# Clearing an idle tile on GpSimd ahead of every sixth gather of a graph network's second layer

## The chip, the cores and the metric

The kernel runs on one core of one Trainium2 chip. The core has five engines that run side by side and wait for each other through semaphores: TensorE (PE; PEld is its weight load), VectorE (DVE), ScalarE (ACT), GpSimd (POOL) and SyncE (SP). Data moves between the off-chip memory and the on-chip memory (SBUF) through 16 DMA engines. A DMA is issued by one of the engines: plain transfers here by SP, gathers and scatters by index (indirect DMAs) by POOL. An engine works through its own instructions strictly in order.

The metric is the device time of one execution in microseconds (us); lower is better.

## The reference

The input is a graph of 10,000 nodes with 768 numbers each and 170,000 edges (80,000 random pairs in both directions, and a self loop for each node), sorted by target. Two layers of graph attention with residual products and normalisations follow, and a last normalisation:

```python
def gat_conv(x, edge_index, W, a_src, a_dst, bias, heads, out_ch, concat):
    ei = _add_self_loops(edge_index, n)
    src, dst = (ei[0], ei[1])
    xl = (x @ W).reshape(n, heads, out_ch)
    alpha_src = jnp.einsum('nhc,hc->nh', xl, a_src)
    alpha_dst = jnp.einsum('nhc,hc->nh', xl, a_dst)
    e = jax.nn.leaky_relu(alpha_src[src] + alpha_dst[dst], 0.2)
    m = jax.ops.segment_max(e, dst, num_segments=n)
    e = jnp.exp(e - m[dst])
    s = jax.ops.segment_sum(e, dst, num_segments=n)
    alpha = e / (s[dst] + 1e-16)
    msg = xl[src] * alpha[:, :, None]
    out = jax.ops.segment_sum(msg, dst, num_segments=n)
    ...
h = gat_conv(x, edge_index, W1, a_src1, a_dst1, b1, HEADS, HID, True)    # 4 heads of 256
h = jax.nn.relu(layer_norm(h, g1, be1))
h = h1 = h + (x @ Wr1 + br1)                                             # 1024 numbers a node
h = gat_conv(h, edge_index, W2, a_src2, a_dst2, b2, 1, OUT_DIM, False)   # 1 head of 768
h = layer_norm(h, g2, be2) + (h1 @ Wr2 + br2)
return _layernorm(x + h)
```

For each node this is a weighted mean over the rows of its neighbours, with weights that depend on both ends of the edge. All of it is in float32.

## The kernel before, in words

**Stages.** First the edges are sorted into lists and the nodes ordered by their number of neighbours, while TensorE makes the table of layer 1 (up to about 950 us). Then layer 1 runs over 79 tiles of 128 nodes and writes each tile's row of table2: 770 numbers a node (768 of the product with W2, two of the attention). Then layer 2 runs over the same 79 tiles and writes the output. The change is in layer 2 alone.

**Slots.** Since nodes of one tile have nearly the same number of neighbours, a tile has SLOTS[t] places of 128 rows, one row for each of its 128 nodes: 41 for the tile with most neighbours, then 27, 26 and so on down to 8. Over all tiles these are TOTAL = 1377 places, numbered q. The tiles' turns go from the short ones up to the 41-slot tile (turn 39) and from 27 down to 9 again. In layer 2 the first place of each tile holds the tile's own rows, which one plain DMA from SP loads (L474); each of the other 1298 is one gather of 128 rows by POOL (L477, in the helper at L445). The places of a tile are its single ones (1 to 4) and blocks of four (a "wave"). Each gather moves 128 x 770 x 4 bytes, 394 KB.

**The ring.** The gathered rows lie in a ring of 41 slots in SBUF. `fetch(upto)` (L471) issues the loads of all places up to a given one, in order. A gather waits until the slot's rows of 41 places earlier have been used.

**One turn of layer 2** (L1077 to L1104), in the order in which it is written out by hand (the schedule is manual, so each engine's instructions run in this order):

1. `exponents(t)`: DVE reads the attention numbers out of the tile's rows (L960 is its first instruction) and ACT takes the exponential (L994).
2. the first part of `norms` of the tile before on DVE (L1048 to L590).
3. `weighed(t)`: DVE makes the weight blocks (`spots`, L1005) and sums the single rows in SBUF (L1014 the first, L1012 the others). L1014 writes one of two row buffers, which the scatter of the tile two turns before must have left.
4. POOL and SP: `ring.fetch` of the places that the singles made free (L1082).
5. second part of `norms` (L601, L603, L604, L1056), which adds the residual product.
6. PE: the blocks of four (`summed`, L1026) between the residual products of the next tile (`residual`, L1036 and L1038).
7. last part of `norms` of the tile before: ACT writes the normalised rows (L1062), POOL scatters them to the output by node number (L1063).
8. POOL and SP: `ring.fetch` of the places that the blocks made free (L1100); SP loads the residual's inputs of the turn after next (L927, L928).

So POOL's queue in layer 2 holds nothing but the gathers (L445), one scatter a tile (L1063) and one small IOTA (L943), in that order: gathers for the singles, the scatter of the tile before, gathers for the blocks.

Of the kernel before, what the change touches and what calls it, by code (L numbers as in the profile page):

```python
# [28 lines left out]
F32 = mybir.dt.float32  # L29
# [6 lines left out]
P = 128  # L36
BANK = 512
# [41 lines left out]
def gnn_kernel(ctx, tc, x, x_cols, src, dst, src_col, dst_col, W1, a_src1, a_dst1, b1, g1, be1, Wr1, br1,  # L79
               W2, a_src2, a_dst2, b2, g2, be2, Wr2, br2, out, n_edges):  # L80
    nc = tc.nc
# [362 lines left out]
    def gather(to, table, index, **more):  # L444
        nc.gpsimd.indirect_dma_start(out=to, out_offset=None, in_=table,  # L445
                                     in_offset=bass.IndirectOffsetOnAxis(ap=index, axis=0), **more)
# [14 lines left out]
    class Ring:  # L461
# [4 lines left out]
        def __init__(self, pool, table, row, size, own, index, more=0):  # L466
            self.table, self.size, self.own, self.issued, self.index = table, size, own, 0, index
            self.row = row
            self.rows = pool.tile([P, size, row + more], F32, name="ring")

        def fetch(self, upto):  # L471
            for q in range(self.issued, min(upto, TOTAL)):
                if q in self.own:
                    nc.sync.dma_start(self.slot(q)[:, :self.row],  # L474
                                      self.table[self.own[q] * P:(self.own[q] + 1) * P, :])
                elif q < self.size or self.own:
                    gather(self.slot(q)[:, :self.row], self.table[:, :], self.index(q))  # L477
                else:
                    gather(self.slot(q)[:, :self.row], self.table[:, :], self.index(q), bounds_check=NP - 1,
                           oob_is_err=False)  # L480
                self.issued = q + 1
# [895 lines left out]
```

## Time and profile before

| | |
|---|---|
| median of 3 runs | 5389.56 us (5383.51 to 5395.65) |
| the profiled execution's own time | 5383.51 us |
| its span, from first to last instruction | 5381.6 us |
| POOL busy | 3296.9 us (61% of the span), 3160 instructions |
| PE / DVE / ACT busy | 4604.0 / 3856.7 / 2741.2 us |
| layer 2: first gather starts, last gather starts, last scatter starts | 3445.03, 5313.94, 5369.81 us |
| moved by DMA in the whole | 1591 MB, mean 296 GB/s |

How to read the lines of the profile shown below. The page cuts the span into 40 equal slices and gives each engine's busy share of a slice in tenths. A table by stage gives the busy time of each engine in a stretch of the span, with the number of instructions in brackets, the clock that TensorE was granted, the share of time that the DMA engines were busy, and what they moved. A group of instructions has its line, engine and operation, the tile written and the tile read, partitions x elements, the count; then busy time and mean ns of one; then the idle time before them and what ended it. The timeline gives start and length of each instruction in us, and in brackets the engine's idle time before it and who released it ("issue": nothing that the profile shows). In the waits, a line reads "who waits <- for whom: us in all, times, longest". Issuing a DMA from POOL counts as busy time of POOL (DMA_INDIRECT); the transfer itself runs on the DMA engines afterwards.

### The profile page before, as it was taken

How to read it: one execution, taken by the hardware profiler on the slowest of the kernel's cores; microseconds unless marked ns; L12 is line 12 of the kernel's file. 1: busy time of each engine (PE TensorE's matmuls, PEld its weight loads, DVE VectorE, ACT ScalarE, POOL GpSimd, SP SyncE). 2: the span in 40 equal slices, each digit the busy share in tenths (PEclk: the TensorE clock that was granted, in tenths of full speed). 3: DMA queues.
4: the chain of work that ended last, by engine and by line, in shares of the span. 5: the costliest groups of instructions: out<-in, count | busy, mean ns of one | idle time of the engine just before them, and what ended most of it. 6: DMA issues, size and time to landing. Idle time of an engine off the chain costs nothing. (4 is left out here: it accounts for less than half of the span.)

```text
span 5381.6 us, 61043 instructions
## 1 busy us (share of the span) xinstructions
PE 4604.0 (86%) x16999; PEld 2427.2 (45%) x16999; DVE 3856.7 (72%) x8213; ACT 2741.2 (51%) x6878; POOL 3296.9 (61%) x3160
## 2 busy tenths in 40 slices
PE   8999996999999887578999999788877766778887
PEld 3444443555555544345555555444433322333343
DVE  5884254899999887788899999577655433465677
ACT  3434443787888876778888888322211111111122
POOL 3446455555666664656666555267777767777774
PEclk9999998999999988789999999899998878889899
DMA  4333625899999996789999999589999989999995
GB/s 155 125 98 88 92 93 213 300 339 345 358 357 368 356 343 248 288 331 346 358 370 354 354 336 321 198 305 359 355 352 352 347 281 343 343 349 356 367 358 224
DMA packets 474309, 1591.47 MB, mean 296 GB/s; under 512 B 118327, under 2 KB 122487, under 8 KB 473958
## 3 DMA queue, kind: packets, MB, share of 16 engines
q0 software_dynamic: 322384, 1286.62, 65.7%
q1 hardware_dynamic: 149520, 297.43, 16.1%
q10 hardware_dynamic: 2054, 3.42, 0.2%
q8 instruction: 137, 2.24, 0.2%
q14 instruction: 214, 1.75, 0.1%
HBM read 1431.80 MB, written 177.29 MB: 299 GB/s over the span
## 5 line engine op out<-in xcount | busy, mean ns | idle before, releaser
L445 POOL DMA_INDIRECT ring<-table,slots x1495 | 1520.0, 1017 | 1012.0 <-issue 230.3
L445 POOL DMA_INDIRECT ring<-table,wide x1180 | 1196.2, 1014 | 387.6 <-issue 189.1
L532 ACT ACTIVATE ring<-ring,e 128x256 f32<-128x256 f32 x3284 | 1337.9, 510 | 0.0
L539 DVE TENSOR_TENSOR acc<-acc,ring 128x1024 f32<-128x1024 f32 x801 | 985.7, 1231 | 79.1 <-ACT ring L532 10.1
L1038 PE MATMUL big<-wr,w 128*128 128x512 f32 (+1 forms) x2464 | 888.0, 509 | 0.0
L179 PE MATMUL big<-w,xT 128*128 128x512 f32 x1896 | 825.7, 597 | 23.3 <-DMA w<-in_W_dram 9.7
L179 PE MATMUL big<-wr,xT 128*128 128x512 f32 x1896 | 833.6, 596 | 0.2 <-ACT xT L715 0.2
L832 PE MATMUL half<-w,hT 128*128 128x512 f32 (+1 forms) x2528 | 830.4, 486 | 0.0
L543 DVE SCALAR_TENSOR_TENSOR acc<-ring,e,acc 128x256 f32<-128x256 f32 x1232 | 602.3, 489 | 82.4 <-PE acc L744 43.0
L1026 PE MATMUL acc<-ring,spots 128*32 128x512 f32 (+1 forms) x4720 | 471.6, 534 | 215.6 <-issue 176.6
L744 PE MATMUL acc<-ring,diagonals 128*128 128x256 f32 x1912 | 483.3, 411 | 200.8 <-ACT diagonals L738 200.5
L1038 PEld LDWEIGHTS big<-wr,w 128*128 128x128 f32 x2464 | 482.1, 198 | 371.6 <-issue 340.6
L832 PEld LDWEIGHTS half<-w,hT 128*128 128x128 f32 x2528 | 477.8, 189 | 372.8 <-issue 310.4
L179 PEld LDWEIGHTS big<-w,xT 128*128 128x128 f32 x1896 | 361.7, 192 | 483.0 <-issue 462.2
L592 ACT ACTIVATE sd<-mv,eps 128x1 f32<-128x1 f32 x237 | 69.8, 295 | 977.5 <-DVE mv L590 977.5
L179 PEld LDWEIGHTS big<-wr,xT 128*128 128x128 f32 x1896 | 356.9, 192 | 420.4 <-issue 419.8
L744 PEld LDWEIGHTS acc<-ring,diagonals 128*128 128x128 f32 x1912 | 390.8, 207 | 285.6 <-ACT diagonals L738 223.4
L1026 PEld LDWEIGHTS acc<-ring,spots 128*32 128x32 f32 x4720 | 148.6, 116 | 553.6 <-issue 464.0
L676 DVE TENSOR_TENSOR scr<-big,ad_b 128x1024 f32<-128x1024 f32 x79 | 96.7, 1224 | 372.9 <-ACT row L673 372.9
L738 ACT ACTIVATE diagonals<-ident,e 128x128 f32<-128x128 f32 x956 | 292.8, 387 | 116.8 <-DVE e L523 116.4
L960 DVE COPY e<-ring 128x15 f32<-128x15 f32 (+22 forms) x110 | 21.9, 200 | 457.4 <-DMA ring<-table,wide 262.3
L681 POOL TENSOR_TENSOR row<-row,none 128x1024 f32<-128x1024 f32 x79 | 187.4, 2372 | 262.3 <-ACT row L673 261.9
(201 smaller groups left out, 4497.2 us busy)
## 6 DMA issues: line engine op xcount, KB each, us to landing
table<-row SPq DMA_DIRECT2D x79, 516.0 KB, 3.6
h_d<-hT SPq DMA_DIRECT2D x79, 512.0 KB, 7.2
w<-h_d SPq DMA_DIRECT2D x77, 512.0 KB, 7.9
table<-row SPq DMA_DIRECT2D x79, 385.0 KB, 6.3
ring<-table SPq DMA_DIRECT2D x79, 385.0 KB, 6.2
xT<-in_x_cols_dram SPq DMA_DIRECT2D x79, 384.0 KB, 4.4
x_d<-xt SPq DMA_DIRECT2D x79, 384.0 KB, 6.6
w<-x_d SPq DMA_DIRECT2D x77, 384.0 KB, 10.3
```

The lines of the kernel that those rows point to most:

```text
L179: nc.tensor.matmul(p[:, c:e], aT[:, j, :], w[:, j, c:e], start=(j == 0), stop=(j == k - 1))
L445: nc.gpsimd.indirect_dma_start(out=to, out_offset=None, in_=table, in_offset=bass.IndirectOffsetOnAxis(ap=index, axis=0), **more)
L532: nc.scalar.activation(row[:, s], row[:, s], AF.Copy, scale=e[:, h:h + 1])
L539: nc.vector.tensor_add(acc[:, :c], acc[:, :c], row[:, :c])
L543: nc.vector.scalar_tensor_tensor(acc[:, s], row[:, s], e[:, h:h + 1], acc[:, s], op0=OP.mult, op1=OP.add)
L676: nc.vector.tensor_mul(m, p[:, :C1], vec)
L681: nc.gpsimd.tensor_add(row[:, :C1], row[:, :C1], b1_b)
L738: nc.scalar.activation(diagonals[:, k * H1 + i, :], ident, AF.Copy, scale=e[:, k, i:i + 1])
L744: nc.tensor.matmul(acc[:, c:d], diagonals[:, k * H1 + i, :], ring.slot(q + k)[:, c:d], start=(k == 0 and c % BANK == 0), stop=(k == m - 1 ...
L832: nc.tensor.matmul(q, hT[:, j, :], w2[:, j, c:c + q.shape[1]], start=(j == 0), stop=(j == K1 - 1))
L1026: nc.tensor.matmul(acc[s, c:d], spots[:, G * j + g, :], ring.slot(q + G * j + g)[:, c:d], start=(j == 0), stop=(j == w - 1), skip_group_ch ...
L1038: nc.tensor.matmul(r[:, c:d], hT[:, j, :], wr2[:, j, c:d], start=False, stop=(j == K1 - 1), skip_group_check=True)
```

## The change

Where the ring is that of layer 2 (its `own` is not empty), it gets one more tile, `idle`, of 128 partitions x 512 float32. In `fetch`, ahead of each place whose number can be divided by six, POOL clears this tile. Nothing reads it. The place itself is then loaded as before, by SP where it is the tile's own rows, else by a gather.

```diff
@@ class Ring, __init__
             self.rows = pool.tile([P, size, row + more], F32, name="ring")
+            if own:
+                self.idle = pool.tile([P, BANK], F32, name="idle")
 
         def fetch(self, upto):
             for q in range(self.issued, min(upto, TOTAL)):
+                if self.own and q % 6 == 0:
+                    nc.gpsimd.memset(self.idle, 0.0)
                 if q in self.own:
                     nc.sync.dma_start(self.slot(q)[:, :self.row],
                                       self.table[self.own[q] * P:(self.own[q] + 1) * P, :])
```

## The prediction

> **What bounds the kernel now.** I read the page's 40 slices first, to see which engine is loaded in the last 14, where layer 2 runs (its first gather starts at 3445.03 us of the span's 5381.6).
>
> ```profile
> POOL 3446455555666664656666555267777767777774
> ...
> DMA  4333625899999996789999999589999989999995
> ```
>
> POOL stands at 7 and the DMA engines at 9, so the DMA looks like the limit and POOL looks free for a quarter of its time. The table by stage (columns: length, busy time and count of PE, PEld, DVE, ACT, POOL, then clock, DMA share, GB/s) corrects that.
>
> ```profile
> core 0: us, PE busy (x) PEld busy (x) DVE busy (x) ACT busy (x) POOL busy (x), PEclk, DMA share, GB/s
> ...
> 3900.00:4380.00 480.00, 372.36 (x1903) 168.18 (x1902) 255.95 (x755) 79.25 (x108) 368.62 (x364) 0.89 0.95 350
> ...
> 4440.00:5060.00 620.00, 469.43 (x2512) 212.20 (x2511) 327.57 (x993) 101.24 (x138) 474.02 (x472) 0.88 0.96 352
> ```
>
> Next, the timeline of POOL in two short windows (start, length, then idle time before it and what ended it):
>
> ```profile
> 3490.76 0.95 POOL L445 DMA_INDIRECT ring<-table,wide  x1 [0.30 <-issue]
> 3491.71 0.16 POOL L943 IOTA number<- 128x1 f32 x1
> 3492.03 0.96 POOL L445 DMA_INDIRECT ring<-table,wide  x1 [0.16 <-issue]
> ...
> 4652.99 0.94 POOL L445 DMA_INDIRECT ring<-table,wide  x1 [0.30 <-issue]
> 4654.24 1.64 POOL L445 DMA_INDIRECT ring<-table,wide  x1 [0.30 <-DMA ring<-table,wide]
> ```
>
> A gather takes 0.95, and 0.30 passes before the next whatever released it: 1.25 us from start to start. In 4440 to 5060 that is 474.0 busy plus 472 x 0.30 = 141.6, together 615.6 of 620 us; in 3900 to 4380, 368.6 + 109.2 = 477.8 of 480. POOL is therefore a queue without a hole, and "7 tenths" is a full engine whose 0.30 isn't counted as busy. Going through POOL's timeline from 3600 to 5314, where the last gather starts, I find one hole above 1.2 us: 24.1 us at 4406 (the 41-slot tile fills the whole ring, and the scatter waits for ACT).
>
> Who waits for POOL is in the waits of DVE between 3900 and 4380, the longest two, and in one tile's hand-over:
>
> ```profile
> DVE e L960 <- DMA ring<-table,slots: 104.2, 10, 14.9
> DVE e L960 <- DMA ring<-table,wide: 56.1, 10, 15.2
> ```
>
> ```profile
> 4773.01 0.95 POOL L445 DMA_INDIRECT ring<-table,wide  x1 [0.30 <-issue]
> ...
> 4777.73 0.18 DVE L960 COPY e<-ring 128x19 f32<-128x19 f32 x1 [7.93 <-DMA ring<-table,wide]
> ```
>
> Here a tile's last gather starts at 4773.01 and its rows are read 4.7 us later, by a DVE that had waited 7.93 us. Matching gathers and tiles by the program's order, that distance stays at 4.5 to 8.6 us over the turns 19 to 61, apart from the 41-slot tile: if transfers piled up, it would grow. So there the rows arrive at POOL's pace. In the shorter tiles on both sides of that stretch (up to 18, and from 63) the ring is ahead, but DVE's first write of a tile (L1014) waits for the scatter of two tiles before (L1063), 90.5 us in all in 36 waits, and that scatter stands in POOL's queue behind the gathers: POOL's pace again, until about 5250, when these waits end. From there, and at the start up to 3600 (where scatters wait 0.95 to 2.2 us for ACT), the tile's own arithmetic sets the pace.
>
> **The change, part by part.** *Allocation.* The idle tile moves the small tiles behind the ring; no instruction of SP, DVE, ACT or PE changes place or waits. The first memset takes over the waits of the first gather (the ends of layer 1), which needs them itself. Cost: nothing; the 59.3 us wait ahead of that gather covers it, and uncovered it would be one memset.
>
> *The memsets.* TOTAL is 1377 places, so q % 6 == 0 gives 230 memsets of 128x512 on POOL, all in layer 2. Each waits only for the memset before it, long done, but behind it stand all later gathers and scatters of POOL. No DMA is added, and SP's loads are not moved past anything.
>
> Length of one, from the groups by shape:
>
> ```profile
> L681 POOL TENSOR_TENSOR row<-row,none 128x1024 f32<-128x1024 f32 x79 | 187.4, 2372 | 262.3 <-ACT row L673 261.9
> ...
> masks.py:197 POOL MEMSET ident<- 128x128 f32 x1 | 0.2, 205 | 0.3 <-POOLq L1369 0.3
> ...
> L1369 POOL MEMSET const-float32-0.0<- 128x1 f32 x1 | 0.1, 99 | 0.2 <-issue 0.2
> ```
>
> 128 columns take 205 ns and one takes 99, so a column costs 106/127 = 0.83 ns, and 512 take 99 + 511 x 0.83 = 0.524 us. The ends: not below the 205 ns of a memset of a quarter of the size; not above half of the two-input L681, 1.19 us. I take 0.524, since it comes from two rows of the same operation and type.
>
> What one delays the queue by is less, because the 0.30 is partly filled. The IOTA above starts the moment the gather ends, and the next gather follows it after 0.16; gather to gather is 1.27 instead of 1.25, for an instruction of 0.16. L681 between gathers of layer 1's preparation behaves likewise: 0.01 after one, 0.15 ahead of the next. So a memset adds 0.524 + 0.16 - 0.30 = 0.384 us. Ends: with the quarter-size row 0.065; with the whole 0.30 kept, 0.524 + 0.30 = 0.82; with half of L681, 1.19 - 0.14 = 1.05.
>
> To this comes what DVE does to POOL. After 3520, 160 gathers take over 1.1 us, together 79.6 us more than 0.95 each (the 1.64 above is one). They follow DVE: of the 97 gathers that overlap a L601, 68 are long, of all about one in eight. Spread over some 1,270 us of POOL's work this is 6.3%; the same share of 0.524 is 0.033. Per memset: 0.384 + 0.033 = 0.417 us.
>
> The Trainium skill's "GPSIMD Engine Reference" (section Key points) gives a reason why this could be worse: POOL shares its SBUF interfaces with VectorE and contends with DVE instructions that read two SBUF inputs or run in a 2-port mode. Estimated by that rule with this case's DVE rows (L1012, L601, L604, L1052 and L1014, about 414 of layer 2's 1862 us, near 1 us each), a memset meets one in some 33% of cases and waits half of it, 0.17 us, and the sum below would rise by 28 us; the gathers' own 6.3% is what I use.
>
> *Where they lie.* By the gather that each precedes, 7 fall before 3517 (POOL waits there 8.6 and 12 us for slots), 9 between 3517 and 3600 (the scatters' waits there, 6 us in excess of 0.30, cover 9 x 0.417 = 3.8), 206 between 3600 and 5250, 8 behind. The 206 lie on the path: 206 x 0.417 = 85.9 us. The hole at 4406 hides none, since it begins with the landing of a gather that the memsets have already made late. Were the covers at the start gone, 16 x 0.417 = 6.7 us would be added. In the last stage the tile's arithmetic sets the pace (15 to 20 us a tile against some 15 to 17 of POOL), so 8 x 0.417 = 3.3 us lie beside it; small waits of scatters between 3600 and 5250 (about 2 us) take back a little. I set these at nothing together.
>
> *Late next.* Each tile of 20 slots gets 3.3 memsets, 1.4 us on 26. DVE, PE and ACT have the slack (DVE busy 328 of 620 us) and only wait longer. The DMA's load falls by 5%.
>
> *Sum.* The profiled execution took 5383.5 us, 1.9 more than its span. 5383.5 + 85.9 = 5469.4. The median of the runs shown, 5389.6, is 6.1 higher, which gives 5475.5. I forecast 5475, 1.6% slower.
>
> **The rivals.** *1. Hidden: the DMA engines set the pace (not slower).* For it: share 0.96, and the gathers could be long because the transfer queue is full. If the 79.6 us of long gathers are such back-pressure, memsets give the queue time to drain and each us of memset shortens a long gather: 85.9 - 79.6 = +6 us, 5396. It decides from about 75 us absorbed. Against it: the long ones follow L601; POOL's waits for landed DMAs in the steady stages don't exceed the usual 0.30 more than a few times; and at the end (5250 to 5320) the engines move 379 GB/s where they move 352 in the steady stage, so about 7% is free, more than the 5% that the memsets take. The Trainium skill's "DMA: Bandwidth & Descriptors" (section Anatomy of one DMA) has 436 GB/s behind a fixed cost; by that estimate a gather of 394 KB needs 0.90 us of transfer, below POOL's 1.25, and this rival falls altogether.
>
> *2. Cheap: the memset runs beside the making of the gather's descriptors.* For it: the IOTA cost only 0.02. Against: that is no more than the filled 0.30 explains. Halfway between 0.02 and 0.417, 0.21 x 206 = 43: 5432.
>
> *3. Dear by DVE.* A memset held as often as DVE's long instructions allow, 0.55 to 0.6 us: 206 x 0.58 = 119, 5509. For it: long gathers exist. Against: L681 takes 2.37 to 2.39 each time with DVE at work.
>
> *4. Nothing filled.* 0.30 stays whole behind the memset: 206 x 0.82 = 169, 5559. Against: both rows of other instructions between gathers.
>
> **How the numbers follow.** The forecast 62%, with a range of its own from 5458 to 5492 (0.33 to 0.50 us a memset). Rival 1 6%, rival 2 9%, rival 3 13%, rival 4 8%; 2% for a gain that I can't name (fewer collisions with DVE than now). The range from 5432 to 5520 holds the forecast, rival 3 and half of rival 2, about 80%. A change under 0.2% (11 us) can't be told from none in runs that spread over 12 us; rival 1 lies there, with a little left to chance: same 5%, faster 2%, slower 93%.
>
> **What would show it.** 230 POOL MEMSET idle at about 0.52 us, starting with no idle time, and the gather behind each 0.16 later; the gather's rows still 0.95 and 0.30; POOL busy up by about 120 us; DMA share in the steady stage down to 0.91 and GB/s to about 335; DVE's waits at L960 for ring longer by some 50 to 60 us; the time from last gather to end no longer than 68 us; layer 1 as before. I am wrong if the memset's row is far from 0.52, if the gathers behind it get shorter (long ones vanish) or start 0.30 after it, or if the steady stages don't grow by about 5%.

## The result, and the profile after

The changed kernel takes 5466.73 us (median of 4 runs, 5465.53 to 5475.59) against 5390.87 for the kernel before (4 runs, 5383.51 to 5395.65): a ratio of 1.0145, interval 1.0128 to 1.0163. That is 76 us, 1.4% slower. The profiled executions, on which the sum of the prediction was made, took 5383.51 and 5466.92 us, with spans of 5381.6 and 5465.1: 83.4 us apart.

All of it lies in layer 2. (Behind the change, kernel lines stand four higher than before: L964 is the old L960, L1042 the old L1038, L1067 the old L1063; the memset is L476.) The first gather starts at 3445.03 us in both traces, the last one at 5313.94 before and 5398.99 after, 85.05 later. From there to the end of the span it takes 67.7 us before and 66.1 after.

The 40 slices of the profile after look like those before: POOL at 7, the DMA engines at 9.

```profile
POOL 2446455555666555556666553477777767777774
...
DMA  4333536899999996899999996799999989999995
```

Nothing in these two rows tells that POOL has 122 us more to do; the span grew with it. The table by stage does, with the two steady stretches cut where they lie after the change (columns as before: length, busy time and count of PE, PEld, DVE, ACT, POOL, then clock, DMA share, GB/s).

```profile
core 0: us, PE busy (x) PEld busy (x) DVE busy (x) ACT busy (x) POOL busy (x), PEclk, DMA share, GB/s
...
3930.00:4430.00 500.00, 368.73 (x1896) 166.67 (x1896) 253.59 (x741) 77.44 (x105) 397.80 (x423) 0.88 0.93 333
...
4495.00:5140.00 645.00, 475.76 (x2444) 215.40 (x2444) 339.93 (x1015) 103.04 (x141) 513.49 (x545) 0.87 0.94 335
```

About the same work of PE, DVE and ACT takes 500 us where it took 480, and 645 where it took 620, 4% more in each. The DMA engines move 333 and 335 GB/s instead of 350 and 352: they wait for POOL.

The group of the memsets among POOL's groups by shape, and four instructions of POOL's timeline:

```profile
L476 POOL MEMSET idle<- 128x512 f32 x230 | 126.8, 551 | 58.8 <-DMA table<-row 58.8
```

```profile
3628.63 0.95 POOL L445 DMA_INDIRECT ring<-table,wide  x1 [0.30 <-issue]
3629.57 0.55 POOL L476 MEMSET idle<- 128x512 f32 x1
3630.28 0.95 POOL L445 DMA_INDIRECT ring<-table,wide  x1 [0.16 <-issue]
3631.54 0.94 POOL L445 DMA_INDIRECT ring<-table,wide  x1 [0.30 <-issue]
```

A memset takes 0.551 us. Only the first has idle time ahead of it (58.8 us, the wait for layer 1); all others start the moment that the gather ends. From the end of one gather to the start of the next it takes 3630.28 - (3628.63 + 0.95) = 0.70 us across a memset and 0.30 without: a memset costs 0.40 us. The median of all is 0.405, put as 0.41 from here on. 206 on the path by 0.41 give 84.5 us.

The starts of the same gathers in both traces show that this accumulates nearly evenly. (Gathers of layer 2 are counted from 0; this table is worked out from the two timelines of POOL.)

| gather | before, us | later by | memsets ahead of it |
|---|---|---|---|
| 0 | 3445.03 | 0.00 | 1 |
| 80 | 3587.55 | 3.52 | 15 |
| 320 | 3933.70 | 18.34 | 58 |
| 640 | 4377.59 | 40.00 | 114 |
| 960 | 4838.34 | 61.40 | 170 |
| 1280 | 5288.50 | 85.79 | 227 |
| 1297, the last | 5313.94 | 85.05 | 230 |

From the 15th memset to the 230th that is 81.5 us for 215, 0.38 each.

### The profile page after: what moved, and what is told of

It reads as the page before. It is cut to its first block, busy times and chain, and to the rows that moved or that the text cites. A ratio compares the mean times of both kernels' runs of the same rounds, so it can differ in the third digit from the quotient of the medians.

```text
span 5465.1 us, 61273 instructions
## 1 busy us (share of the span) xinstructions
PE 4627.2 (85%) x16999; PEld 2435.4 (45%) x16999; DVE 3876.9 (71%) x8213; ACT 2741.6 (50%) x6878; POOL 3418.4 (63%) x3390
## 5 line engine op out<-in xcount | busy, mean ns | idle before, releaser
L1042 PE MATMUL big<-wr,w 128*128 128x512 f32 (+1 forms) x2464 | 899.5, 514 | 0.0
L1042 PEld LDWEIGHTS big<-wr,w 128*128 128x128 f32 x2464 | 488.9, 201 | 385.4 <-issue 354.4
L964 DVE COPY e<-ring 128x15 f32<-128x15 f32 (+22 forms) x110 | 25.0, 229 | 490.3 <-DMA ring<-table,wide 288.7
L1040 PE MATMUL big<-w,ident 128*128 128x512 f32 (+1 forms) x308 | 172.3, 647 | 221.2 <-issue 127.1
```

The source lines that it names most:

```text
L1040: nc.tensor.matmul(r[:, c:d], ident, xt[:, c:d], start=True, stop=False, skip_group_check=True)
L1042: nc.tensor.matmul(r[:, c:d], hT[:, j, :], wr2[:, j, c:d], start=False, stop=(j == K1 - 1), skip_group_check=True)
```

## The experiments

The theory was the prediction's: POOL is a full queue, a memset adds its own length and a start of 0.17 us less the 0.30 that it fills, and nothing on another engine counts. The rivals: a price that does not depend on the memset's size; a pace set by the DMA engines' bytes; and contention with DVE. The kernel before took 5386 us on some chips and 5743 on others, so each run below is compared with the kernel before on its own chip; the runs of the slower chips come last.

### A quarter of the tile

```diff
-                self.idle = pool.tile([P, BANK], F32, name="idle")
+                self.idle = pool.tile([P, P], F32, name="idle")
```

> The change with the idle tile cut from 128x512 to 128x128; the 230 memsets stay where they are. Theory (POOL's queue sets layer 2's pace, and a memset delays it by its own length + 0.17 - 0.30): a memset of 0.205 us costs 0.075, times the 206 that lie on the path 15 us, so about 5407 against 5391 before. Rival (any instruction put between two gathers breaks their chain at a fixed price, 0.41 us as with 512 columns): 5475 again. Rival (DMA sets the pace and the 76 us came otherwise): no change of a size that follows the columns.

Measured: 5414.96 us (4 runs) against 5385.92 (18 runs), ratio 1.0051 (1.0034 to 1.0068), 29 us more. POOL's group:

```profile
L476 POOL MEMSET idle<- 128x128 f32 x230 | 52.2, 227 | 58.8 <-DMA table<-row 58.7
```

Across a memset a gather now follows 0.39 us after the one before, 0.09 more than without; 206 times that is 18.5 us. The last gather starts 28.8 us later than before. The other 10 us are gathers and scatters of over 1.1 us: after 3520 they hold 90.05 us beyond 0.95 each, and 79.6 in the kernel before. So the number of memsets does not set the cost, their length does: the fixed price falls. The expected 15 us are missed, by 3.5 for the longer memset (0.227 us, not 0.205) and by the 10 of longer gathers, whose cause I did not find.

### The same memsets on DVE

```diff
-                    nc.gpsimd.memset(self.idle, 0.0)
+                    nc.vector.memset(self.idle, 0.0)
```

> The same 230 memsets of 128x512 at the same places of the program, but on DVE. Theory (only POOL's queue matters in the middle): POOL's gathers stand at 1.25 us again, DVE hides the memsets in its waits for gathered rows, and only those in the first and last tiles, some 26 x 0.5 us, can show: 5391 to 5405. Rival (writing this much into SBUF beside the gathers is what costs): again about +76, 5467.

Measured: 5392.78 us (10 runs), ratio 1.0012 (1.0003 to 1.0021), 7 us more, within the expected 5391 to 5405.

```profile
L476 DVE MEMSET idle<- 128x512 f32 x230 | 111.5, 485 | 27.1 <-DVE idle L476 18.7 <-DMA ring<-table,wide 2.1 <-DMA ring<-table,slots 0.3
```

DVE takes 111.5 us more in layer 2, nearly as much as POOL took, and the time moves by 7: DVE has slack, POOL has none. It also shows that the new tile in SBUF and the 230 writes to it cost next to nothing by themselves.

The Trainium skill's "GPSIMD Engine Reference" (section Key points) says that for elementwise work DVE is structurally about twice as fast. The two rows here show less for a memset: 485 ns on DVE and 551 on POOL, a factor of 1.14.

### A tiny memset ahead of every gather

```diff
-                self.idle = pool.tile([P, BANK], F32, name="idle")
+                self.idle = pool.tile([P, 1], F32, name="idle")
...
-                if self.own and q % 6 == 0:
+                if self.own and q not in self.own:
```

> A memset of 128x1 on POOL ahead of every one of the 1298 gathers of layer 2, in place of the 128x512 ahead of every sixth place. Theory, by the rows of the changed kernel (0.17 us between a memset's end and the next gather, 0.30 between two gathers): 0.10 + 0.17 = 0.27 takes the place of 0.30, so the queue gets faster by 0.03 x 1180 = 35 us, 5356; by the IOTA's row of the kernel before (0.16 + 0.16) it gets slower by 0.02 each, 24 us, 5415. Rival (a fixed price of 0.41 for each interruption): +480, 5870.

Measured: 5404.92 us (7 runs), ratio 1.0031 (1.002 to 1.0042), 19 us more, for 1298 memsets. The group, and POOL's timeline:

```profile
L476 POOL MEMSET idle<- 128x1 f32 x1298 | 159.5, 123 | 59.1 <-DMA table<-row 58.7
```

```profile
4640.20 0.12 POOL L476 MEMSET idle<- 128x1 f32 x1
4640.51 0.94 POOL L445 DMA_INDIRECT ring<-table,wide  x1 [0.19 <-issue]
4641.44 0.12 POOL L476 MEMSET idle<- 128x1 f32 x1
4641.76 0.95 POOL L445 DMA_INDIRECT ring<-table,wide  x1 [0.19 <-issue]
...
4647.45 0.11 POOL L476 MEMSET idle<- 128x1 f32 x1
4648.92 0.95 POOL L445 DMA_INDIRECT ring<-table,wide  x1 [1.35 <-PE acc L1030]
```

0.12 + 0.19 = 0.31 takes the place of 0.30. So 1298 instructions on the full engine cost next to nothing as long as they fit into the idle 0.30. The 35 us that the expectation had gained are missed, since it took 0.10 + 0.17; the IOTA's 0.16 + 0.16 was nearer. A cost of 0.4 us an instruction would have been over 500 us. The 19 us come from something else: the last line is one of twelve holes, which the section at the end tells of.

### Half the bytes

```diff
-                elif q < self.size or self.own:
+                elif self.own:
+                    gather(self.slot(q)[:, :HALF], self.table[:, :].rearrange("n (a b) -> (n a) b", b=HALF), self.index(q))
+                elif q < self.size:
                     gather(self.slot(q)[:, :self.row], self.table[:, :], self.index(q))
```

It starts from the kernel before (HALF = 385 of 770); a line not shown sets the other half of the ring's rows to zero once.

> The kernel before, without any memset, in which each gather of layer 2 brings 385 of a row's 770 numbers (half the bytes, from another place of the table), and the rest of the ring is cleared once at the start of layer 2. It leaves out half of the rows' data, so its output is not the reference's. Theory (POOL's making of the gathers sets the pace): a gather still starts every 1.25 us, the steady stages take as long as before, the total lies within 5365 to 5395, and the DMA share falls from 0.96 to 0.6 or less. Rival (the DMA engines set the pace): layer 2's steady stages shrink with the bytes, by a third or more, to a total of 4800 to 4950.

Measured: 5341.73 us (2 runs) against 5385.92, ratio 0.9915 (0.9896 to 0.9934), 44 us less. By stage, and the longest waits of DVE in the first of these stretches:

```profile
3900.00:4380.00 480.00, 376.13 (x1953) 170.72 (x1952) 259.78 (x787) 81.35 (x111) 367.82 (x366) 0.89 0.69 207
...
4440.00:5040.00 600.00, 454.89 (x2340) 208.56 (x2332) 314.23 (x948) 96.81 (x132) 460.80 (x458) 0.88 0.69 209
```

```profile
DVE w L1052 <- PE acc L1030: 156.2, 18, 14.2
DVE w L1018 <- DMA out_dram<-w,order: 28.4, 9, 8.5
```

The DMA engines fall from 350 to 207 GB/s, and POOL issues 366 instructions in 480 us where it issued 364: its pace is 1.25 us a gather for half the bytes too. The total lies 23 us below the expected 5365 to 5395, and the DMA share of 0.69 above the expected 0.6. Of the 44 us some 30 lie in the holes of POOL and 4 behind the last gather: the hole of 24.1 us at the 41-slot tile shrinks to 0.96, which puts the gathers from 14.8 us ahead at gather 640 to 35.9 at gather 720, and 9 us are won by gather 160, where POOL's small waits for landed transfers are gone and its scatters wait for ACT 0.95 us instead of 7.3. (The early waits for slots stay: 15.5 and 6.8 us, before 12.0 and 8.6.) The attention numbers, at the end of the row, are not gathered here, so DVE's waits at the exponents (160 us in that stretch before) are gone too and come back behind the blocks on PE. The rival that the bytes set the pace falls: it needed some 400 us and more. Long gathers and scatters stay too (79 us in excess after 3520, against 79.6), so these are not a sign of a full transfer queue.

The Trainium skill's "DMA: Bandwidth & Descriptors" (section Anatomy of one DMA) has a transfer grow with its bytes at 436 GB/s behind a fixed cost; the estimate by it, 0.90 us for a whole row block and 0.45 for half, both below 1.25, agrees with a pace that did not move.

### Every third place

```diff
-                if self.own and q % 6 == 0:
+                if self.own and q % 3 == 0:
```

> The change with 128x512 memsets ahead of every third place, 459 of them. Theory: 412 on the path by 0.41 us, 169 us, the same as twice the size: 5545 to 5575. If each interruption had a price of its own beside the length, this would cost more than the doubled size by 206 times that price.

> 128x512 memsets ahead of every third place, 459 of them, again. On a chip where the kernel before takes about 5390 us: 412 on the path by 0.41 us, 169 us, so 5545 to 5575; more than that if each interruption has a price of its own beside its length. On a chip where it takes about 5740: near 5670, as with the doubled tile, since as much time is put between the gathers.

Measured on a chip where the kernel before takes 5385.76 us (9 runs): 5553.31 (2 runs), ratio 1.0313 (1.0294 to 1.0331), 168 us more.

```profile
L476 POOL MEMSET idle<- 128x512 f32 x459 | 252.6, 550 | 59.0 <-DMA table<-row 58.9
```

412 on the path by 0.41 are 169 us, as expected: the price of one memset is the same when there are twice as many. (Against the 76 us of the changed kernel it is 2.2 times; the intervals, 69 to 88 and 158 to 178 us, leave room for twice.) The other run of the same kernel, on a slower chip, is told of below.

### Memsets only where the prediction saw cover

```diff
-                if self.own and q % 6 == 0:
+                if self.own and (q < 96 or q > 1320) and q % 2 == 0:
```

48 memsets at the start of layer 2 and 28 at its end.

> Memsets of 128x512 only where the tile's own arithmetic was found to set the pace: ahead of each second place below 96 and above 1320, 76 of them, none between. Theory: 0.41 us each delays the gathers there, but the 14 before the first tiles run and most of the 28 at the end are covered; the 34 in the early tiles meet some 6 us of cover: the time rises by 3 to 12 us, 5389 to 5398. Rival (every memset costs its 0.41 wherever it stands): 76 x 0.41 = 31 us, 5417.

> 128x512 memsets only ahead of each second place below 96 and above 1320, 76 of them, again. On a chip where the kernel before takes about 5390 us: most are covered, the time rises by 3 to 12 us; by the rival (each costs 0.41 wherever it stands) by 31 us. On a chip where it takes about 5740: no change, since nothing is spaced in the middle.

Measured on the chip with 5385.76 us before: 5406.16 (5 runs), ratio 1.0036 (1.0023 to 1.005), 20 us more: beyond the theory's 3 to 12, short of the rival's full price. The starts of the gathers, set against the trace of before, place it: 9.6 us are lost from gather 0 to gather 80, with 45 of the memsets, which is half of 45 x 0.41; then 3.7 us more up to gather 1200, with only three memsets on the way. From gather 1200 to the last one 11.05 us are lost, with 28 memsets: 0.39 each, the full price. POOL's timeline near the end shows why:

```profile
5330.18 1.35 POOL L445 DMA_INDIRECT ring<-table,wide  x1 [0.17 <-issue]
...
5339.30 0.95 POOL L445 DMA_INDIRECT ring<-table,wide  x1 [0.17 <-DVE inv L1054]
5340.55 1.01 POOL L1067 DMA_INDIRECT out_dram<-w,order  x1 [0.30 <-issue]
```

In the kernel before, scatters in this stage still wait 0.69 or 0.96 us for ACT; here the scatter starts 0.30 after the gather, with no wait. The cover at the end was a few tenths of a us a tile, and the memsets used it up: POOL was the limit again. The tail gave 2.6 us of it back (65.1 us instead of 67.7).

### On slower chips

Six runs fell on two chips on which the kernel before takes 5742.60 us (23 runs) and 5742.78 (7 runs). All kernels of this section are compared with these. The first of the two chips ran the kernels of the last two sections, and these:

```diff
-                self.idle = pool.tile([P, BANK], F32, name="idle")
+                self.idle = pool.tile([P, 2 * BANK], F32, name="idle")
```

> The change with the idle tile doubled to 128x1024. Theory (POOL's queue; price = length + 0.17 - 0.30): by the rows of 128 and 512 columns (0.227 and 0.551) a memset takes 0.98, costs 0.85, times 206 gives 175 us: about 5560, with the last gather 175 to 195 us later than before. Rival (a price for each interruption): 5466. Rival (the first memsets only eat into spare time of the DMA engines): more than double of the 76 to 81 us of the change, above 5570.

The second is half the bytes together with the change's memsets:

> The change on top of half_rows: each gather of layer 2 brings 385 numbers a row, and the 230 memsets of 128x512 are there. It leaves out half of the rows' data, so its output is not the reference's. Theory: the memsets cost what they cost with whole rows, since the DMA engines have no part in it: 5342 of half_rows and 80 to 90 more, 5422 to 5432. Rival (the price came from a DMA queue near its limit): clearly less than 76, below 5400.

The other chip ran the double-sized tile again, and the changed kernel itself:

> The doubled idle tile (128x1024) again, beside the change itself. Where the kernel before takes about 5390 us, POOL's queue paces layer 2: 0.98 + 0.17 - 0.30 = 0.85 us for each of 206 memsets, 175 us, about 5562. Where it takes about 5740 (the chip of the last four runs, on which TensorE's instructions come late in layer 2), it is again faster than before, near 5670. Rival (a price for each interruption): as the change itself.

> The changed kernel, unaltered, on the same chip as the doubled tile. Where the kernel before takes about 5390 us: 206 x 0.41 = 85 us more than before, half of what the doubled tile adds. Where it takes about 5740: between before and the doubled tile, 5690 to 5720, if the spacing of the gathers is what helps there.

| kernel | chip | us (runs) | ratio (interval) |
|---|---|---|---|
| every third place | first | 5672.40 (2) | 0.9864 (0.9824 to 0.9904) |
| double tile | first | 5669.16 (2) | 0.9858 (0.9819 to 0.9898) |
| ends only | first | 5745.82 (12) | 0.9997 (0.998 to 1.0014) |
| half rows with memsets | first | 5762.10 (8) | 1.0026 (0.9996 to 1.0055) |
| double tile | second | 5669.56 (2) | 0.987 (0.9843 to 0.9898) |
| the changed kernel | second | 5711.51 (5) | 0.9948 (0.9929 to 0.9967) |

On these chips the change makes the kernel 31 us faster, and more memsets make it faster still. The doubled tile never ran on a faster chip. Two expectations made for a full POOL queue (double tile and every third place, first chip) are missed in sign, because POOL is not full there. The two made after these runs, near 5670 for the double tile and 5690 to 5720 for the changed kernel, are met, but they carried on what had been seen and name no mechanism. What half rows with memsets was to decide stays open, since half rows alone did not run on such a chip. In the trace of ends only, which takes as long as the kernel before, POOL waits for ACT at the scatters:

```profile
POOL out_dram L1067 <- ACT w L1066: 174.8, 41, 22.6
```

In the kernel before, on the chip of its profile, that wait is 26.7 us in 4 times (both from 3600 to 5300 us). DVE in turn waits ahead of its first reading of PE's blocks (L1052, the old L1048). First two waits in ends only, then the one of the kernel before; "remote" means that the profile names no instruction as releaser:

```profile
DVE w L1052 <- remote: 468.7, 34, 20.4
...
DVE w L1052 <- PE big L1042: 112.3, 9, 21.7
```

```profile
DVE w L1048 <- PE acc L1026: 87.9, 39, 6.1
```

And PE's timeline in ends only shows matmuls that come one or two at a time:

```profile
4635.58 0.38 PE L1042 MATMUL big<-wr,w 128*128 128x256 f32 x1 [0.24 <-issue]
4637.01 0.59 PE L1042 MATMUL big<-wr,w 128*128 128x256 f32 x2 [1.06 <-issue]
4638.45 0.38 PE L1042 MATMUL big<-wr,w 128*128 128x256 f32 x1 [0.85 <-issue]
4639.85 0.69 PE L1042 MATMUL big<-wr,w 128*128 128x256 f32 x1 [1.02 <-issue]
```

The trace of before has them (here of 512 columns) as unbroken rows:

```profile
4635.86 3.60 PE L1038 MATMUL big<-wr,w 128*128 128x512 f32 x8
4639.38 1.51 PE L1026 MATMUL acc<-ring,spots 128*32 128x512 f32 x16
4640.82 3.70 PE L1038 MATMUL big<-wr,w 128*128 128x512 f32 x8
```

The granted clock is lower in ends only, 0.83 against 0.89 from 3600 to 5300 us. It does not slow the matmuls themselves: unbroken rows of eight with 512 columns take 3.11 us from first start to last start in the median of both traces.

The same work can be compared across the traces, from gather 90 to gather 1280. POOL's holes are what its pauses of over 0.4 us hold beyond 0.30; PE's gaps are those of 0.3 to 3 us for which the profile names no releaser. (Worked out from the timelines.)

| trace | chip | gather 90 to 1280, us | POOL's holes, us (times) | PE's gaps, us (times) |
|---|---|---|---|---|
| kernel before | faster | 1683.9 | 27 (8) | 34 (17) |
| the changed kernel | faster | 1766.2 | 24 (3) | 35 (16) |
| ends only | slower | 2049.2 | 391 (157) | 187 (183) |
| half rows with memsets | slower | 2057.9 | 322 (106) | 158 (191) |
| the changed kernel | slower | 1978.0 | 241 (110) | 147 (193) |
| double tile, second chip | slower | 1941.4 | 128 (50) | 90 (111) |

What follows. On the slower chips POOL has holes, and the holes are the loss: ends only takes 365 us more than the kernel before on the faster chip, and its holes hold 364 more. The changed kernel takes 294 more there: 213 in holes, and the rest is as much as its memsets cost on the faster chip, 82 (1766.2 - 1683.9). So by this sum the memsets are not hidden; they cost their price, and at the same time the holes shrink by 150 us. Why they shrink is not shown. The gain goes with fewer gaps on PE, as if POOL's pauses let TensorE's instructions through, but the gaps are less than half of the loss, and half rows with memsets has fewer gaps than ends only and a longer time. That kernel also speaks against the bytes as the brake, though its waits are others. Why the instructions come late on some chips, and why spacing the gathers helps, stays open.

## Why the prediction came out right

It had 5475 us, 5432 to 5520, slower at 93%. Measured: 5466.7. By its steps:

- **POOL is a full queue in layer 2, the "7 tenths" are a full engine.** Right on the chips of the profile, and shown: memsets on POOL cost 76 us, the same memsets on DVE 7; half the bytes leave the pace of 1.25 us as it was.
- **The length, 0.524 us.** It measured 0.551. With the other sizes (123 ns for one column, 227 for 128, 973 for 1024) a column costs 0.82 to 0.84 ns; the slope of 0.83 was right, the start was 0.02 too low.
- **0.30 partly filled, 0.16 behind the memset.** Right: 0.17. This was the step that decided most. Rival 4 (the 0.30 stays, 5559 us) falls with the row of the gather behind the memset, and again with the tiny memsets. Rival 2 (beside the gather's making, 5432) falls with the same row: the next gather starts 0.70 us after the last one, not 0.30.
- **0.033 a memset for collisions with DVE.** Not there as such. The median memset takes 0.54 against a mean of 0.55, and only 5 of 230 take over 0.6, so collisions make some 0.01. The missing 0.03 of length and 0.01 of start made up for it: that 0.417 met 0.41 is luck. Rival 3 falls, and the estimate of 28 us from the Trainium skill's "GPSIMD Engine Reference" (section Key points: POOL shares its SBUF interfaces with VectorE) with it: these 230 memsets show no such price.
- **206 on the path, 24 covered.** Right in the sum, 85.05 us at the last gather against 85.9, and in part by luck. From gather 90 to gather 1250, the stretch of the 206, 204 memsets made 78.5 us; the 26 outside made 6.5, where nothing was predicted. Up to gather 80, 15 memsets cost 3.5 us. In the end stage the cover is thinner than I took it: of the 3.3 us set at nothing, the tail gave 1.6 back, and with a dense row of memsets there (ends only) each cost 0.39. The step that failed is "the tile's arithmetic sets the pace" behind 5250: it does so by a few tenths of a us a tile. Long gathers and scatters went the other way: 76.1 us in excess in 160, 3.5 less than before; in gathers alone it is 71.2 against 78.1.
- **The hole at 4406 hides none.** Nearly: 24.1 us before, 23.3 after.
- **The bytes don't set the pace** (against rival 1). Right, by the run with half the bytes, in which the long gathers did not go away either.
- **The sum.** 5383.5 + 85.9 = 5469.4 against 5466.9 for the profiled execution. To that I added 6.1 us, since the profile of before stood below its median; the profile of after stands at its own (5466.92 and 5466.73), so that step put 6 of the 9 us of error in.
- **What would show it.** The steady stages grow by 4% (about 5% predicted), POOL's busy time is up by 121.5 us (120 predicted), the GB/s fall to 333 and 335 (335), the tail is 66.1 us (at most 68). The DMA share falls to 0.93 or 0.94, not to 0.91. DVE's waits at the exponents for ring rows rise less than the 50 to 60 us predicted:

```profile
DVE e L964 <- DMA ring<-table,wide: 93.1, 12, 16.5
DVE e L964 <- DMA ring<-table,slots: 79.7, 8, 15.8
```

These are 172.8 us in the stretch from 3930 to 4430, 12.5 more than in the matching one before; from 4495 to 5140 they are 248.8, against 231.9 from 4440 to 5060. That is 29 us of the 45 by which the two stretches are longer. DVE's whole idle time in them rose by 35 us (from 224.1 to 246.4, and from 292.4 to 305.1), and the rest is work: the later stretch after holds 1015 instructions of DVE where that of before holds 993, because the two weren't cut at the same instruction.

What the prediction did not foresee is that its first premise belongs to the chip: on the slower chips, where PE is late, POOL isn't full, and the sign turns.

## What to carry to other kernels

An engine that issues indirect DMAs can be full at seven tenths busy: add the pause after each issue before calling it free. Into that pause a short instruction goes at next to no cost (0.01 us for one of 0.12), and a longer one costs what stands out of it, here its length less 0.13 us, as long as the queue is full; so price it at the place where it stands, and move it to an engine with slack rather than make it cheaper. A cover of a few tenths of a us a tile is used up by the first instructions that are put under it. And whether the queue is full can differ from chip to chip, so measure before and after on the same one.

## What the runs showed of the hardware that I had not expected

**A hole at every 106th indirect DMA.** With a tiny memset ahead of each gather, twelve gathers start 1.35 to 2.55 us after what stands before them instead of 0.19: at 3632.5, 3778.8, 3920.9 us and so on to 5214.2. Counted from 0 over all indirect DMAs of POOL in layer 2 they are numbers 115, 221, 327 and so on up to 1281, 106 apart without exception. Their excess is 21.6 us, as much as that kernel's 19. In the kernel before, the same numbers start after 0.30, three of them after 0.40, 0.81 and 1.12; with the memsets on DVE the longest is 1.85. What happens at every 106th, and why the tiny memsets make it longer, is not known.

**Long gathers differ between kernels for no reason that I found.** The excess of gathers and scatters over 1.1 us, after 3520 us, is 79.6 us before, 76.1 after, 86.2 with the memsets on DVE and 90.05 with the small tile on POOL. That is 10 us that a sum of instructions can't give.

**One kernel, two speeds by chip.** The kernel before takes 5386 to 5391 us in three of the comparisons and 5743 in the two others, 6.6% more. In the trace of ends only, the first gather of layer 2 starts at 3451.95 us, 7 us later than in the trace of before; the rest of the difference is in layer 2. A change that costs 1.4% on the one kind gives 0.5% on the other.
